# Attention's loop on Trainium2: a chunk's loads issued one a slot, those of an inverse one a step

## The chip, the cores and the metric

The kernel runs on one core of a Trainium2 chip. The metric is the device time of one execution in microseconds (us); the median of several executions is compared. A core has a matrix engine (TensorE, PE in the profile, with its weight loads as PEld), VectorE (DVE), ScalarE (ACT), GpSimd (POOL) and SyncE (SP), which here only issues DMAs. Each engine takes its instructions in the order of its own list and waits on semaphores for the others.

## The reference

Two layers, each an attention part and an MLP whose outputs are multiplied and added to the residual. The change lies in the first layer's attention, a gated delta rule over 1024 steps, for 2 sequences of 16 heads of 128:

```python
q, k, v = (silu(causal_dwconv(x @ W)) for each)      # k scaled by 128 ** -0.5
alpha, beta = sigmoid(x @ Wa + ba), sigmoid(x @ Wb + bb)
def step(S, inps):
    qt, kt, vt, at, bt = inps
    Sk  = einsum('bhvk,bhk->bhv', S, kt)
    err = Sk - vt
    S   = at[..., None, None] * S - bt[..., None, None] * (err[..., None] * kt[:, :, None, :])
    ot  = einsum('bhvk,bhk->bhv', S, qt)
    return (S, ot)
o = layernorm_over_128(o) * ln_w + ln_b
return (o * sigmoid(x @ Wg)) @ Wo
...
x = x + s * silu(ffn(xn))          # the first layer's end; a second layer follows
```

## The kernel before, in words

**Chunks.** The recurrence is done in 8 chunks of 128 steps. Four streams (two heads of two sequences, `NS`) form a head group `hg`, 8 of them; a unit is one head group and one chunk, 64 units in all, in an order that alternates two head groups. Within a chunk a unit lower triangular matrix has to be inverted. It is done by 32x32 diagonal blocks: `invert` loads those of all chunks of one head group into `ll` (four DMAs of 128 KB, in pieces of 32 numbers), sets `ml` to the identity (two POOL memsets), eliminates in 31 steps of two DVE instructions each (`tl`, then `ml`), copies the result back into `ll` in four ACT copies, and stores it with four DMAs. It is a generator: each `next` of it does one step.

**The loop.** After a front part (layernorm, the first MLP, the first three head groups' keys and decays, about 400 us) the loop `for u in range(len(units) + 1)` runs the units. `weave` cuts each unit into 10 slots (`LINKS`): a slot advances one of two chains (`across` of this unit or of the one before), runs what is due, and gives the wide projections (`made`, `ahead_k`) and the small products of `within` and `ahead_l` to the matrix engine up to a share of their summed cost. `later(n, *steps)` puts its steps off: the first by n slots, each following one by one slot more. Outside the loop it runs them at once.

**Order.** In the loop the instructions of PE, DVE, ACT and POOL are kept in the order in which the program writes them (`Ordered`). Those of `nc.sync`, all DMAs, are not: a scheduler places them into SP's list when the program is built, so that moving one in the source need not move it by as much in the list. SP's list is one list: a DMA whose semaphore has not come holds up all DMAs behind it, and each DMA also waits for the one eight places ahead of it to land.

**What a unit loads.** `within`, called for the next unit at the start of each, issues one DMA each for `kb` (keys), four for `ground` (the `G` blocks, the inverses, 40 KB each in pieces of 32 numbers), one for `eb` (decays) and one for `eg` (row decays, broadcast). `eg` and `kb` are read by POOL's products `kg` and `qg`, five slots later; `eb` by DVE's `kd` and `at`; `ground` by PE's products `zw` in the chain one unit later. The chain itself goes pks, `rt` (DVE), pr, `rr` (ACT), and then four times `zw` into `w` (ACT), with `rr` reduced by DVE in between; each `w` is turned into `wt` by four small DMAs (16 KB), the last by DVE copies. `pst` needs all of `wt`, and makes the next `state`.

**The inverse in the loop.** Every 8 units an inverse is started (u = 0, 8, 16, 24, 32, 40), and its steps are taken at fixed slots of 7 of the 8 units: four in the first unit (slots 0, 7, 8, 9), six in each other one (slots 0, 2, 4, 5, 7, 9), 40 in all:

```python
if u % 8 < 7:
    for k in (0, 2, 4, 5, 7, 9) if u % 8 else (0, 7, 8, 9):
        later(k + 1, lambda steps=steps: next(steps, None))
```

Before the change all four loads of `ll` and the memsets fall to the first step, two steps do nothing, and the elimination begins in the fourth.

Of the kernel before, what the change touches and what calls it, by code (L numbers as in the profile page):

```python
# [22 lines left out]
P = 128  # L23
# [7 lines left out]
NS = 4  # L31
# [25 lines left out]
def cols(ap, n):  # L57

    if len(ap.shape) == 2:
        ap = ap.unsqueeze(2)  # L60
    return ap.to_broadcast([ap.shape[0], ap.shape[1], n])
# [246 lines left out]
def first_layer(ctx, tc, a, cst, minus_half, keep, xnT, od, gd, pd, then):  # L308
# [29 lines left out]
    nc = tc.nc  # L338
# [223 lines left out]
    gr, egr = (dr.tile([NCOL, P], F32, name=n, bufs=1) for n in ("gr", "egr"))  # L562
# [10 lines left out]
    def rows(src, hg, c, dst):  # L573

        col = c * H * B + hg * NS
        nc.sync.dma_start(
            dst, src[col : col + NS, :].rearrange("s t -> (s t)").unsqueeze(0).to_broadcast([P, NS * P])
            .rearrange("p (s t) -> p s t", s=NS)
        )
# [6 lines left out]
    order = {"loop": False, "slot": 0}  # L586
# [6 lines left out]
    def later(n, *steps):  # L593


        for i, step in enumerate(steps):
            if order["loop"] and n + i:
                due.setdefault(order["slot"] + n + i, []).append(step)
            else:
                step()  # L600

    def mm(out, **kw):
        PE.matmul(out, **kw)

    def turn(out, src):
        PE.transpose(out, src, ident)
# [136 lines left out]
    def invert(hg, store):  # L743

        ll = pl.tile([P, 32, 32], F32, tag="ll", name=f"ll_{hg}")
        for bl in range(4):
            nc.sync.dma_start(
                ll[32 * bl : 32 * bl + 32],
                store["l"][:, :, :, SLOT[bl], :].rearrange("c s i t -> (c s) i t"),
            )  # L750
        m = pl.tile([P, 32, 32], F32, tag="ml", name=f"ml_{hg}")
        POOL.memset(m, 0.0)
        POOL.memset(m.rearrange("p i j -> p (i j)")[:, 0 : 32 * 32 : 33], 1.0)
        for _ in range(3):
            yield
        for i in range(31):
            shape = [P, 31 - i, i + 1]
            t = pl.tile([P, 256], F32, tag="tl", name=f"tl_{hg}_{i}", bufs=2)
            tv = t[:, : (31 - i) * (i + 1)].rearrange("p (t j) -> p t j", j=i + 1)
            DVE.tensor_tensor(  # L760
                tv,
                ll[:, i, i + 1 :].unsqueeze(2).to_broadcast(shape),
                m[:, i, : i + 1].unsqueeze(1).to_broadcast(shape),
                ALU.mult,
            )
            rest = m[:, i + 1 :, : i + 1]
            DVE.tensor_tensor(rest, rest, tv, ALU.subtract)
            yield

        for i in range(0, 32, 8):  # L770
            ACT.copy(ll[:, :, i : i + 8].rearrange("p j i -> p i j"), m[:, i : i + 8])
            yield
        for bl in range(4):
            nc.sync.dma_start(
                store["l"][:, :, :, SLOT[bl], :].rearrange("c s j i -> (c s) j i"),
                ll[32 * bl : 32 * bl + 32],
            )
        yield

    def within(hg, c, store):  # L780

        u = f"{hg}_{c}"
        half = slice((c % 2) * P, (c % 2 + 1) * P)
        q = windows[hg, c // 2]["q"][:, :, half]
        k = pools["b"].tile([P, NS, P], F32, tag="kb", name=f"kb_{u}")
        nc.sync.dma_start(k, store["k"][c // 2][:, :, half])
        G = pools["g"][:, units.index((hg, c)) % 3]
        for s in range(NS):
            r = slice(32 * s, 32 * s + 32)
            nc.sync.dma_start(G[r, :, r], store["l"][c, s])  # L790
        e = pools["b"].tile([P, NS, P], F32, tag="eb", name=f"eb_{u}", bufs=1)
        nc.sync.dma_start(e, store["e"][c])

        eg = pools["b"].tile([P, NS, P + 4], F32, tag="eg", name=f"eg_{u}", bufs=3)
        POOL.memset(eg[:, :, 0:1], 1.0)
        rows(egr, hg, c, eg[:, :, 1 : P + 1])
        kg = pools["b"].tile([P, NS, P], F32, tag="kg", name=f"kg_{u}")
        qg = pools["b"].tile([P, NS, P], F32, tag="qg", name=f"qg_{u}", bufs=3)
        later(
            5,  # L800
            lambda: POOL.tensor_tensor(kg, k, eg[:, :, 0:P], ALU.mult),
            lambda: POOL.tensor_tensor(qg, q, eg[:, :, 1 : P + 1], ALU.mult),
        )
        yield 0
        pk = pools["i"].tile([P, NS, P], F32, tag="pi", name=f"pk_{u}")
        for s in range(NS):
            turn(pk[:, s, :], k[:, s, :])

        kd = pools["b"].tile([P, NS, P], F32, tag="kd", name=f"kd_{u}", bufs=3)
        later(1, lambda: DVE.tensor_tensor(kd, pk, cols(e[:, :, P - 1 : P], P), ALU.mult))  # L810
        yield 4 * TURN

        pqk = pools["a"].tile([P, NS, P], F32, tag="pa", name=f"pqk_{u}")
        for s in range(NS):
            mm(pqk[:, s, :], lhsT=k[:, s, :], rhs=q[:, s, :], start=True, stop=True)
        at = pools["b"].tile([P, NS, P], F32, tag="at", name=f"at_{u}", bufs=3)
        later(1, lambda: DVE.tensor_tensor(at, pqk, e, ALU.mult))
        parts[hg, c] = eg, qg, kg, at, kd, G
        yield 4 * NARROW
# [156 lines left out]
    for hg in range(3):  # L976
        stores[hg] = new_store(hg)
        wk = load_weights(hg, ("wk",))
        steps = invert(hg - 1, stores[hg - 1]) if hg else iter(())
        for p in range(NP):  # L980
            for step in of_e:
                step()
            some(1)
            done(ahead_k(hg, p, wk["wk"], stores[hg]))
            loads, *of_e = ahead_e(hg, p, stores[hg])
            of_e = itertools.chain(*of_e)
            for step in loads:
                step()
            some(1)
            ell()  # L990
            for _ in zip(range(0 if hg and not p else 14), steps):
                pass
            ls.append((hg, p))
# [52 lines left out]
    with tc.issue_after(last["act"].ins):  # L1046
# [3 lines left out]
        done(made(0, 0, "v"))  # L1050
        done(made(1, 0, "q"))
        done(within(0, 0, stores[0]))
        halves = sorted(pd)

# [56 lines left out]
        for u in range(len(units) + 1):  # L1111
# [15 lines left out]
            if u % 8 == 0:  # L1127
                steps = invert(slot + 2, stores[slot + 2]) if slot + 2 < HG else none
                if slot + 3 < HG:
                    wk = load_weights(slot + 3, ("wk",))  # L1130
                    stores[slot + 3] = new_store(slot + 3)
# [12 lines left out]
            if u + 1 < len(units):  # L1144
                hg, c = units[u + 1]
                ready = within(hg, c, stores[hg])
                other(ready, 1)
# [4 lines left out]
            if turn4 in (0, 2) and ls:  # L1152
                hg, i_ = ls[turn4 // 2]
# [599 lines left out]
```

## Time and profile before

| what | value |
|---|---|
| median of 3 runs | 3177.61 us (3177.41 to 3177.93) |
| profiled execution | 3174.2 us, of which the span 3172.4 us |
| granted TensorE clock, mean | 0.999 |
| PE busy in the span | 3138.0 us |
| attention's loop in the trace | about 400 to 1825 us |
| DMAs of SP in the loop, per unit | 12 of `wt`, 4 of `ground`, one each of `kb`, `eb`, `eg` and others |

The span is the time from the first to the last instruction of the profiled execution. In the rows of the profile, nearly all lines are L132, the helper through which ordered instructions pass; so they are told apart by their tiles, written out<-in. PE's busy time is modelled at its end and says how long it was occupied, not how well; a wait is read from the idle time before an instruction and from what ended it.

### The profile page before, as it was taken

Reading aid. Unit: us, or ns where it says so; the run is one execution under the profiler, and the core shown is the slowest. Engines: PE = TensorE matmul, PEld = TensorE weight load, DVE = VectorE, ACT = ScalarE, POOL = GpSimd, SP = SyncE. Lnnn points to the kernel's source line nnn. Section 1 sums busy time; section 2 is a strip of 40 time slices with the busy share of each in tenths; the row PEclk is TensorE's granted clock in tenths of the full one; section 3 lists DMA queues with packets and bytes.
Section 4 is the critical chain, followed back from the end, with each engine's and each line's share of the span. In section 5 each row is a group of like instructions: output and inputs, shape, how many; then the busy total and the mean of one; then the engine's idle time right before and its main releaser. Section 6 shows DMA issues by size and latency. Waiting matters only on the chain.

```text
span 3172.4 us, 38119 instructions
## 1 busy us (share of the span) xinstructions
PE 3138.0 (99%) x12390; PEld 1941.4 (61%) x12390; DVE 2148.2 (68%) x4294; ACT 1251.4 (39%) x2269; POOL 833.4 (26%) x1210
## 2 busy tenths in 40 slices
PE   8999999999999999999999999999999999999998
PEld 7577756666666666666666644555555555555554
DVE  5557678786877868675545455677777666776677
ACT  3476555546555555534433311222222222322223
POOL 2000122222222222322222210333333333333322
PEclk9999999999999999999999999999999999999999
DMA  6244344444444543443334364100011001010014
GB/s 184 63 119 113 104 132 119 112 131 126 122 108 129 142 122 105 111 133 101 89 89 137 112 212 155 31 30 27 27 33 34 27 27 34 27 33 27 27 37 133
DMA packets 499751, 287.40 MB, mean 91 GB/s; under 512 B 207585, under 2 KB 440801, under 8 KB 499553
## 3 DMA queue, kind: packets, MB, share of 16 engines
q1 hardware_dynamic: 490688, 268.97, 30.0%
q0 software_dynamic: 6560, 11.80, 1.3%
q10 hardware_dynamic: 2304, 4.20, 0.4%
q8 instruction: 99, 1.62, 0.2%
q14 instruction: 100, 0.81, 0.1%
HBM read 183.90 MB, written 88.34 MB: 86 GB/s over the span
## 4 chain that ended last, share of the span: by engine, by line
PE 89%; DVE 5%; ACT 2%; issue 2%; DMA 1%; SPq 1%; POOL 0%; DVEq 0%; ACTq 0%; POOLq 0%
PE po L132 18%; PE pua L132 7%; PE pga L132 7%; PE pwk L132 6%; PE pgate L132 6%; PE pwv L132 5%; PE pwq L132 5%; PE jpo L211 4%; PE zw L132 4%; PE puc L132 3%; PE pgc L132 3%; PE pu L132 3%; PE pg L132 3%; PE pr L132 2%; PE pub L132 2%; PE pgb L132 2%
## 5 line engine op out<-in xcount | busy, mean ns | idle before, releaser
L132 DVE TENSOR_TENSOR acc<-acc,po 128x512 f32<-128x512 f32 x408 | 278.2, 682 | 208.3 <-PE po L132 207.6
L132 PEld LDWEIGHTS po<-w_d,i 128*128 128x128 f32 x1024 | 194.5, 190 | 142.6 <-issue 111.2
L132 PE MATMUL po<-w_d,i 128*128 128x256 f32 (+1 forms) x1024 | 275.4, 392 | 0.0
L132 PE MATMUL pgate<-xnT,wg 128*128 128x512 f32 x512 | 245.8, 593 | 0.2 <-ACT q L132 0.2
L132 PE MATMUL pwq<-xnT,wq 128*128 128x512 f32 x512 | 245.2, 594 | 0.0
L132 PE MATMUL pwv<-xnT,wv 128*128 128x512 f32 x512 | 243.0, 593 | 1.8 <-ACT gate L132 1.8
L132 PE MATMUL pua<-xq,w_u 128*128 128x512 f32 x512 | 240.6, 592 | 0.0
L132 PE MATMUL pga<-xq,w_g 128*128 128x512 f32 x512 | 240.6, 592 | 0.0
L132 PE MATMUL pwk<-xnT,wk 128*128 128x512 f32 x512 | 236.1, 593 | 1.7 <-ACT ka L132 1.7
L132 ACT COPY g<-pga 128x512 f32<-128x512 f32 x96 | 56.2, 585 | 445.8 <-PE pga L132 438.5
L132 DVE SCALAR_TENSOR_TENSOR v<-prewv,cw,v 128x512 f32<-128x512 f32 x192 | 166.3, 867 | 62.5 <-ACT v L132 53.1
L132 PEld LDWEIGHTS po<-w_d,s 128*128 128x128 f32 x720 | 136.8, 190 | 95.4 <-issue 76.8
L132 ACT COPY w<-zw 128x128 f32<-128x128 f32 x192 | 50.6, 264 | 356.7 <-PE zw L132 356.5
L132 DVE TENSOR_TENSOR rr<-rr,zw 128x128 f32<-128x128 f32 x192 | 54.8, 285 | 197.3 <-PE zw L132 193.3
L132 PE MATMUL po<-w_d,s 128*128 128x256 f32 x720 | 184.8, 379 | 0.0
L132 ACT ACT_TABLE_LOAD x133 | 170.6, 1283 | 17.8 <-PE pr L132 11.3
L132 POOL TENSOR_TENSOR rs<-rs,minus_half 128x4 f32<-128x4 f32 x64 | 64.5, 1007 | 427.0 <-DVE rs L132 409.2
L132 POOL TENSOR_TENSOR ot<-ot,gate 128x512 f32<-128x512 f32 x64 | 86.3, 1348 | 338.0 <-ACT ot L132 308.3
L132 DVE SCALAR_TENSOR_TENSOR ka<-prewk,cw,ka 128x512 f32<-128x512 f32 x192 | 149.6, 781 | 33.8 <-ACT ka L132 23.2
L132 PEld LDWEIGHTS zw<-rr,ground 128*128 128x128 f32 x512 | 96.5, 190 | 123.9 <-issue 102.4
L132 DVE SCALAR_TENSOR_TENSOR q<-prewq,cw,q 128x512 f32<-128x512 f32 x192 | 159.1, 829 | 15.7 <-POOL eg L132 7.3
L132 PEld LDWEIGHTS zw<-w,ground 128*128 128x128 f32 x768 | 110.9, 191 | 66.0 <-issue 55.4
(248 smaller groups left out, 6647.2 us busy)
## 6 DMA issues: line engine op xcount, KB each, us to landing
e<-gr SPq DMA_DIRECT2D x64, 256.0 KB, 3.9
de<-e SPq DMA_DIRECT2D x64, 256.0 KB, 2.9
dk<-ka SPq DMA_DIRECT2D x32, 512.0 KB, 2.8
kb<-dk SPq DMA_DIRECT2D x64, 256.0 KB, 3.4
eb<-de SPq DMA_DIRECT2D x64, 256.0 KB, 3.0
eg<-egr SPq DMA_DIRECT2D x64, 256.0 KB, 3.9
od<-ot SPq DMA_DIRECT2D x64, 256.0 KB, 2.1
wt<-w SPq DMA_DIRECT2D x768, 16.0 KB, 2.0
```

The costliest lines, as they stand in the source:

```text
L132: i = getattr(self.engine, name)(*args, **kw)
L211: matmul(po, lhsT=ot[:, h, :], rhs=self.wo[h], start=(h == h0), stop=(h == H - 1))
```

## The change

In `within`, `kb` stays where it was; the loads of `eg`, `eb` and the four of `ground` are put off to one a slot, in this order, from the next slot on. In `invert`, when it runs in the loop, each of the four loads of `ll` is a step of its own, and the empty steps go; the memsets fall to the step of the first elimination, the fifth, and everything after it comes one step later than before. Outside the loop nothing changes. In the diff no line of the output projection is touched.

```diff
@@ invert @@
                 ll[32 * bl : 32 * bl + 32],
                 store["l"][:, :, :, SLOT[bl], :].rearrange("c s i t -> (c s) i t"),
             )
+            if order["loop"]:
+                yield
         m = pl.tile([P, 32, 32], F32, tag="ml", name=f"ml_{hg}")
         POOL.memset(m, 0.0)
         POOL.memset(m.rearrange("p i j -> p (i j)")[:, 0 : 32 * 32 : 33], 1.0)
-        for _ in range(3):
+        for _ in range(0 if order["loop"] else 3):
             yield
@@ within @@
-        for s in range(NS):
+        e = pools["b"].tile([P, NS, P], F32, tag="eb", name=f"eb_{u}", bufs=1)
+
+        eg = pools["b"].tile([P, NS, P + 4], F32, tag="eg", name=f"eg_{u}", bufs=3)
+        POOL.memset(eg[:, :, 0:1], 1.0)
+
+        def block(s):
             r = slice(32 * s, 32 * s + 32)
             nc.sync.dma_start(G[r, :, r], store["l"][c, s])
-        e = pools["b"].tile([P, NS, P], F32, tag="eb", name=f"eb_{u}", bufs=1)
-        nc.sync.dma_start(e, store["e"][c])
-
-        eg = pools["b"].tile([P, NS, P + 4], F32, tag="eg", name=f"eg_{u}", bufs=3)
-        POOL.memset(eg[:, :, 0:1], 1.0)
-        rows(egr, hg, c, eg[:, :, 1 : P + 1])
+
+        later(
+            1,
+            lambda: rows(egr, hg, c, eg[:, :, 1 : P + 1]),
+            lambda: nc.sync.dma_start(e, store["e"][c]),
+            *(functools.partial(block, s) for s in range(NS)),
+        )
```

## The prediction

> **What bounds the kernel now.** I read the page first, then the window sums, then PE's waits, then the order of time around the longest of them.
>
> The page says that the matrix engine is never free: PE is busy 99% of the span, and 89% of the chain that ended last is PE's.
>
> ```profile
> PE 3138.0 (99%) x12390; PEld 1941.4 (61%) x12390; DVE 2148.2 (68%) x4294; ACT 1251.4 (39%) x2269; POOL 833.4 (26%) x1210
> PE 89%; DVE 5%; ACT 2%; issue 2%; DMA 1%; SPq 1%; POOL 0%; DVEq 0%; ACTq 0%; POOLq 0%
> ```
>
> The window sums give the loop (400 to 1825 us) by itself; the columns are busy us of PE, PEld, DVE, ACT, POOL.
>
> ```profile
> 400.00:1825.00 1425.00, 1411.22 (x6766) 909.58 (x6765) 986.77 (x2429) 698.47 (x1423) 385.34 (x664) 1.00 0.43 117
> ```
>
> So PE was idle 1425.0 - 1411.2 = 13.8 us there. Busy PE can hide a wait, so I also took the distance from each matmul's start to the next, less the median of its shape (429 ns for 128x512, 111 ns for 128x128): 27.6 us in excess over the loop, of which 17 us lie in places of over 0.15 us. That is a ceiling: a change that leaves PE's list alone cannot win more than 27 us (0.9%). And it does leave it alone: with buffer numbers left out, the built program has the same list on PE. PE's waits in the loop say what little is to be had:
>
> ```profile
> PE pst L132 <- DMA wt<-w: 3.5, 1, 3.5
> PE pst L132 <- DVE wt L132: 2.9, 3, 1.7
> PE pwv L132 <- ACT gate L132: 1.8, 3, 0.6
> PE zw L132 <- ACT w L132: 1.7, 4, 1.1
> PE zw L132 <- DVE rr L132: 1.0, 3, 0.5
> ```
>
> One of them is a DMA's. It is at u = 40, where an inverse starts and the unit is short because no keys are prepared any more. SP's and PE's timelines there (start, duration, what):
>
> ```profile
> 1315.84 1.84 SPq L735 DMA_DIRECT2D dl<-lt  x4
> 1318.30 2.71 SPq L747 DMA_DIRECT2D ll<-dl  x4
> 1321.06 2.97 SPq L790 DMA_DIRECT2D ground<-dl  x4
> 1324.12 0.55 SPq L792 DMA_DIRECT2D eb<-de  x1
> 1324.72 0.43 SPq L576 DMA_DIRECT2D eg<-egr  x1
> 1325.25 4.97 SPq L868 DMA_DIRECT2D wt<-w  x8
> ...
> 1328.87 1.13 PE L132 MATMUL pst<-wt,kd 128*128 128x128 f32 x8 [3.52 <-DMA wt<-w]
> ```
>
> ACT's `w` for the first of these `wt` was ready at 1317.4, but its DMAs stood behind fourteen others until 1325.25: PE stood from 1325.4 to 1328.9. At the starts of u = 8 to 32 the same queue forms, but PE has more other work and waits for no DMA.
>
> **The change part by part.** Each DMA costs SP about 0.6 us of issue, wherever it stands; none is added or taken away. In the built program's order SP has 2122 DMAs as before.
>
> *SP's order at an inverse's start.* At u = 40 it becomes: four `dl`, one `ll`, `kb`, `eg`, `eb`, four `wt`, three `ground`, four `wt`, `ll`, `ground`, two `ll`. From the row above: first `ll` issued by 1318.9, then three DMAs, so `wt` from about 1320.7 to 1323.1, landing (2.0 us median) by 1325.1, when PE wants it at 1325.6. The wait for the DMA goes. What is late next is `wt`'s last quarter, which DVE copies: in the trace these copies end at 1326.3, behind two taps that wait for ACT until 1323.45. `pst` would start at 1326.3 and not 1328.87: 2.6 us. But `eg` lands at about 1324 and not 1328.6, and so POOL's `kg` starts then, beside the second of those taps.
>
> *A rule that speaks against the change.* DVE at the place of PE's longest wait for DVE (`wt`, 1.84 us at 1236.5), with POOL beside it:
>
> ```profile
> 1233.52 0.37 DVE L132 TENSOR_TENSOR ml<-ml,tl 128x207 f32<-128x207 f32 x1
> 1235.56 2.86 DVE L132 SCALAR_TENSOR_TENSOR v<-prewv,cw,v 128x512 f32<-128x512 f32 x2 [1.67 <-ACT v L132]
> 1238.45 1.25 DVE L132 COPY wt<-zw 32x128 f32<-32x128 f32 x4
> ...
> 1235.08 1.29 POOL L132 TENSOR_TENSOR kg<-kb,eg 128x512 f32<-128x512 f32 x1
> 1236.32 1.55 POOL L132 TENSOR_TENSOR qg<-q,eg 128x512 f32<-128x512 f32 x1
> ```
>
> Two taps take 2.86 us, where two take 1.54 with POOL free (1323.45). Of the loop's 504 taps the 401 with no large POOL product beside them take 0.76 us at most; the 103 with one have a median of 1.17. [...] I take 0.6 (half a pair's loss, since the tap may have begun first): 2.0 us is left.
>
> *The loads of a unit elsewhere.* `eg` comes earlier in SP's list in 28 units, by up to 10 places, because it no longer stands behind `ground`; `ground` comes later for 101 of its 256 DMAs, by up to 20; `kb` later in 15 units, by up to 6; `wt` earlier for 188 of 768. Set at the times of their new places, `ground` still lands 8.7 us or more ahead of the first `zw` that reads it, `eb` 4.9 ahead of `kd`, `kb` 3.5 ahead of its reader. So these cost nothing; the cover is that slack, and without it PE's `zw` would wait by what is missing. POOL's waits show what the earlier `eg` is worth on POOL:
>
> ```profile
> POOL kg L132 <- DMA eg<-egr: 24.2, 10, 6.8
> ```
>
> Yet nobody waits for `kg`: PE's list of waits has none. Worth 0, except by the collisions, which move in ten units and can fall well or badly.
>
> *The inverse.* Its first elimination comes one step later and its loads three steps later. Two DVE instructions (0.39 us at 612.0) leave the place ahead of `rr`; PE waited there for `rr` at 794.1 (0.70 us) and 435.5 (0.23): -0.4 and -0.2. They go to behind `at`, ahead of `rt` at u = 8, 24, 40; ahead of them other DVE work is shorter by as much, so `rt` is not later by them. But the fourth `ll` now lands shortly before. At u = 8 and 24 it is issued at 611.2 and 972.1 at the latest (the `wt` before it at its old time, then five DMAs), and lands 3.9 us after its issue began: 615.1 and 976.0, with `at` over at 615.9 and 976.7. No wait. At u = 40: `wt` until 1327.5, then four DMAs, issued from 1329.5, landed by 1333.4 to 1334; there `at` is over, with the 2.0 us gained, at about 1334. A wait of 0 to 1.8 us, and `rt` with PE's `pr` right behind: I take +0.3. [...] At u = 16 and 32 the fourth load may be some tenths late, but no `rt` follows there.
>
> The two memsets (1.17 us of POOL) move 15 places, behind a copy that ends at 611.5 at u = 8, so they are over by 612.7, ahead of 615.9: 0. Without that gap of 3 us DVE, with `rt` behind, would wait for POOL. ACT's four copies at an inverse's end (0.65 us each) come one step later, and the four stores up to 5 places later; PE has no wait of over 0.15 us in those units, and the stores are read over a unit later: 0, with ±0.6 for each of six if an ACT copy hits a `w`.
>
> **Sum.** -2.0 (u = 40) - 0.6 (`rr`) + 0.3 (`ll`) = -2.3 us. The profiled execution is 3174.2 us (span 3172.4 and 1.8 around it) and would become 3171.9. The median is 3177.6, 3.4 above it; the same step gives 3175.3.
>
> **The rivals.** About 0.2% (6.4 us) is what a measurement of this kernel can tell from no change, so the forecast is "within".
>
> *More is won (faster).* If `wt` early and POOL free early ease the DVE waits also, most of the 17 us in single places is open: u = 40 with its whole 3.7, the 1.8 at 1236, 0.9 at 1409, 0.7 at 1751 and the start's 1.0 make 8.1: 3169.5. For it: `kg` waited for a DMA ten times, and `wt` moves forward. Against: the waits for ACT (`gate`, `w`) repeat at fixed places that SP does not touch, and at 1236 SP's order is unchanged.
>
> *Collisions (slower).* `kg` and `qg`, started earlier in units where `eg` was late, fall on taps ahead of `wt` copies, as at 1236. Price: 1.8 us each by that row. It decides from five such units on (5 x 1.8 - 2.3 = +6.9 us); with all ten it is +16: 3193. With six, 3186. Against: DVE is idle 438 of 1425 us in the loop, and only taps in front of a PE wait count.
>
> *It does nothing.* SP's scheduler had already pulled the old loads apart in most units; then only u = 40 changes, and if the taps collide there, the result is 3177.6.
>
> **How the numbers follow.** The likeliest case with the third rival, 0.60: 3171.5 to 3183. More is won by over 6.4 us, 0.17. Collisions, or an ACT or `ll` wait I have undersized, by over 6.4 us, 0.23. The range for 8 in 10 is 3168 to 3186: it takes in part of both outer cases.
>
> **What would show it.** Right: no PE wait for `wt`'s DMA near 1325, `pst` there at about 1327, `kg<-eg` waits well below 24 us, PE's idle time in the loop near 12 us. Wrong: a DVE wait for `ll` at the first `tl` of u = 8 or 24, new PE waits for `wt` copies or `rr` with a tap of over 1 us ahead of them, or PE waiting for `ground`.

## The result, and the profile after

| | before | after |
|---|---|---|
| median, runs of the first comparison (20 each) | 3177.47 us (3173.73 to 3180.52) | 3171.31 us (3169.64 to 3173.70) |
| ratio | | 0.9985 [0.9979, 0.9990] |
| profiled execution | 3174.2 us (span 3172.4) | 3172.0 us (span 3170.2) |
| all runs with a granted clock on record | 3176.12 (n = 110, standard deviation 1.95) | 3171.36 (n = 31, 1.20) |

The 110 are without before's 20 of the first comparison, whose clock is not on record; with them its median is 3176.17. So the change makes the kernel faster by 6.2 us in the first comparison and by 4.8 us over all runs (interval 4.0 to 5.5). The forecast was 3175.3 us, 2.3 us below before. The first thing to see is that the two profiled executions differ by 2.2 us only, nearly the forecast. The one of before, at 3174.2, is a short one: of 130 executions of that kernel 17 are shorter. The question was therefore twofold: are the steps of the sum where they were said to be, and where do the other 2.5 to 4 us come from, which this pair of profiles doesn't show?

On the page of after PE's busy time is 3136.5 us, 1.5 less, and its share stays 99%.

The window sums of after give the loop: PE idle 1425.0 - 1412.8 = 12.2 us, where 12 had been forecast.

```profile
400.00:1825.00 1425.00, 1412.79 (x6774) 911.60 (x6773) 992.52 (x2439) 698.14 (x1423) 383.58 (x666) 1.00 0.43 118
```

PE's waits in the loop of after (what waits, for what: us in total, times, longest). The wait for the DMA of `wt`, 3.5 us, is gone. DVE's copies have one wait more (4.7 in 4, it was 2.9 in 3), and `w` has 3.5 us in 7, where it had 1.7 in 4.

```profile
PE pst L132 <- DVE wt L132: 4.7, 4, 1.7
PE zw L132 <- ACT w L132: 3.5, 7, 1.1
```

**u = 40.** The timeline of after there (start, duration). SP's order is the one forecast. `wt` is issued from 1320.26, and `pst` starts at 1326.86, where it had waited until 1328.87. But `eg` lands at about 1323, so `kg` and `qg` now run beside the two taps (a tap is a DVE instruction that adds one step of the causal convolution), which take 3.20 us and not 1.54. What PE waits for, 1.74 us, is the `wt` copies behind these taps.

```profile
1320.26 2.44 SPq L876 DMA_DIRECT2D wt<-w  x4
...
1323.29 3.20 DVE L132 SCALAR_TENSOR_TENSOR v<-prewv,cw,v 128x512 f32<-128x512 f32 x2 [3.02 <-ACT v L132]
...
1323.16 1.28 POOL L132 TENSOR_TENSOR kg<-kb,eg 128x512 f32<-128x512 f32 x1 [0.33 <-DMA eg<-egr]
1324.40 1.54 POOL L132 TENSOR_TENSOR qg<-q,eg 128x512 f32<-128x512 f32 x1
...
1326.86 1.46 PE L132 MATMUL pst<-wt,kd 128*128 128x128 f32 x8 [1.74 <-DVE wt L132]
```

**u = 32.** Here the change made a wait that was not there. The timeline of after: `kg` starts 5.6 us earlier than in before (1148.33 there, after a wait of 3.96 us for `eg`) and meets a pair of taps, which take 2.81 us instead of 1.54. `w` then comes late, and PE's `zw` waits for it.

```profile
1142.78 1.30 POOL L132 TENSOR_TENSOR kg<-kb,eg 128x512 f32<-128x512 f32 x1
...
1143.32 2.81 DVE L132 SCALAR_TENSOR_TENSOR v<-prewv,cw,v 128x512 f32<-128x512 f32 x2 [2.36 <-ACT v L132]
...
1151.27 0.71 PE L132 MATMUL zw<-w,ground 128*128 128x128 f32 x4 [1.10 <-ACT w L132]
```

**The drift.** PE's list is the same in both kernels, so each product of one can be set against the same product of the other. The difference of their start times, after less before, is the drift; where it steps, time was won or lost. The table has the steps of three profiled executions of the changed kernel's lists against the one of before; the third has two waits filled, as told below. Negative is faster.

| stretch of the loop (us) | what | after | after again | after filled |
|---|---|---|---|---|
| 419 to 425 | `pr`, first unit | -0.24 | -0.98 | -1.06 |
| 425 to 440 | `rr` at 436 | -0.33 | -0.33 | -0.33 |
| 440 to 690 | `rr` at 442, `pr` at 687 | -0.75 | -0.73 | -0.75 |
| 790 to 800 | `rr` at 795 | -0.80 | -0.81 | -0.81 |
| 800 to 850 | sundry | -0.63 | -0.62 | -0.62 |
| 1140 to 1155 | `zw` for `w`, u = 32 | +1.27 | +1.26 | +1.26 |
| 1239 to 1245 | behind the wait of u = 36 | 0.00 | +1.33 | +0.01 |
| 1245 to 1326 | ending in `pst`, u = 40 | -1.71 | -2.37 | -2.07 |
| stretches not listed, in sum | | +0.21 | +0.40 | +0.42 |
| whole loop (395 to 1830) | | -2.98 | -2.85 | -3.95 |

Most steps repeat to 0.02 us from one execution to the next. Three do not: the first unit's, u = 40's, and one of 1.33 us at 1240, behind a wait that both kernels have. The experiments are about these. Executions differ ahead of the loop too, in kernels with and without the change: by -1.0 to +1.0 us at 395 against the first one of before. After had +0.5 there and +0.3 behind the loop, which is why the two profiles differ by 2.2 us and their loops by 3.0.

### The profile page after: what moved, and what is told of

Same layout as the page of the kernel before. It is cut to its first block, busy times and chain, and to the rows that moved or that the text cites. A ratio compares the mean times of both kernels' runs of the same rounds, so it can differ in the third digit from the quotient of the medians.

```text
span 3170.2 us, 38109 instructions
## 1 busy us (share of the span) xinstructions
PE 3136.5 (99%) x12390; PEld 1941.8 (61%) x12390; DVE 2151.2 (68%) x4294; ACT 1251.1 (39%) x2269; POOL 830.9 (26%) x1210
## 4 chain that ended last, share of the span: by engine, by line
PE 88%; DVE 5%; issue 2%; ACT 2%; DMA 2%; SPq 1%; POOL 0%; DVEq 0%; ACTq 0%; POOLq 0%
PE po L132 17%; PE pua L132 7%; PE pga L132 7%; PE pgate L132 6%; PE pwk L132 6%; PE pwq L132 5%; PE pwv L132 5%; PE jpo L211 4%; PE zw L132 4%; PE puc L132 3%; PE pgc L132 3%; PE pu L132 3%; PE pg L132 3%; PE pr L132 2%; PE pub L132 2%
```

## The experiments

The kernels ran in three groups of four, each on a chip of its own and with its own runs of before: medians 3176.05, 3176.13 and 3175.79 us (33 runs each).

### The two kernels again

> The kernel before, unchanged, for its profile. Its first profiled execution took 3174.2 us, 3.3 below its median of 3177.5, and stood only 2.2 us of span above the one of the changed kernel, while the medians are 6.2 apart. If the missing 4 us are waits that the kernel before has in most executions and missed in that one, a profiled execution near 3177.5 shows them as steps of PE's drift against the changed kernel, most likely at the starts of an inverse (u = 8 to 40), where SP's queue is longest. If they lie outside the loop (front, second layer), the steps stand before 400 or behind 1825 us, and the change has nothing to do with them. Time: ratio 1.000 to the kernel before.

> The changed kernel, unchanged, on the same chip as the others: 0.9985 of the kernel before, and a profile with pst at u = 40 waiting for DVE's wt (about 1.9 us) and not for a DMA, and the wait for w at u = 32 (1.26 us) again, since both come from the order of kg and the taps and not from chance.

Measured: before 3176.45 us, ratio to its neighbours 1.0001 [0.9992, 1.0010]; after 3171.42, 0.9986 [0.9978, 0.9995]. The difference is there again, 4.6 to 5 us, and the profile of before was 3176.9 this time, 2.7 us above the first. This second profile shows where an ordinary execution of before is longer. The window sums of before over the stretch behind the wait of u = 40, and then of before again over those behind u = 36 and u = 40; the third column from the right is PE's granted clock, which the first profile of before has at 1.00 behind u = 36 too.

```profile
1328.00:1336.00 8.00, 7.13 (x55) 6.39 (x56) 5.87 (x13) 1.32 (x2) 4.37 (x6) 1.00 0.25 75
```

```profile
1236.00:1243.00 7.00, 5.32 (x17) 3.07 (x17) 6.38 (x16) 2.88 (x4) 2.18 (x5) 0.76 0.43 103
1328.00:1336.00 8.00, 6.82 (x35) 6.85 (x36) 4.66 (x12) 0.97 (x2) 3.91 (x6) 0.57 0.30 86
```

The clock's records in that trace say the same: half of full speed for 3.4 us from 1239.7 and for 6.8 us from 1328.4. In the timeline of before again `pst` takes 2.05 us behind the wait, where the row shown of before has 1.13, though nothing in the lists has changed:

```profile
1329.18 2.05 PE L132 MATMUL pst<-wt,kd 128*128 128x128 f32 x8 [3.48 <-DMA wt<-w]
```

The drift of this execution against the first one of before grows by 1.34 us at 1240 and by 2.25 us between 1326 and 1340. The first profile of before had the same two waits (1.68 and 3.52 us) and no half clock behind either: whether a wait draws one differs from one execution to the next, and no run here shows what decides it. Of the 11 profiles of this study in which the wait at u = 36 is as it was (1.67 to 1.73 us), four have half clock for 3.4 us behind it. Over the loop, the first profile of before was the lucky one.

### One part of the change alone

Only what `within` does; in `invert` the old order stands:

```diff
-            if order["loop"]:
-                yield
...
-        for _ in range(0 if order["loop"] else 3):
+        for _ in range(3):
```

> Only the loads of a chunk are put off; the inverse's four loads stay in one step. At u = 40 wt stands behind four dl, four ll, kb, eg and eb and is issued from about 1322.9 on, landed by 1327.2; eg lands near 1326, behind the two taps, so kg does not meet them: pst at about 1327.2 (1328.87 before, 1326.86 with the whole change in the trace's own times). The new wait of 1.26 us at u = 32 (kg beside the taps) stays if eg lands before 1145 there. Theory of the queue: 2 to 4 us of the 6 us. Rival, that the loads of ll are what counts: nothing.

Measured: 3172.22 us, ratio 0.9989 [0.9980, 0.9998], 3.9 us below all runs of before (interval 2.0 to 5.3). `pst` at u = 40 starts at 1325.49, after a wait of 1.83 us, and `kg`, at 1324.50, comes behind the pair of taps, as expected. The profile names DVE's `wt` as what ended the wait, but those copies were over at 1324.57. The first of the `wt` DMAs, issued at 1321.07, landed at 1325.41: what is left is still a wait for a DMA. The step at 1151 is there (+1.13), and the `rr` step at 795 is smaller (-0.4 over 790 to 800).

Only what `invert` does; in `within` the old order stands:

```diff
-        later(
-            1,
-            lambda: rows(egr, hg, c, eg[:, :, 1 : P + 1]),
-            lambda: nc.sync.dma_start(e, store["e"][c]),
-            *(functools.partial(block, s) for s in range(NS)),
-        )
+        for s in range(NS):
+            r = slice(32 * s, 32 * s + 32)
+            nc.sync.dma_start(G[r, :, r], store["l"][c, s])
+        nc.sync.dma_start(e, store["e"][c])
+        rows(egr, hg, c, eg[:, :, 1 : P + 1])
```

> Only the inverse's loads are spread and its steps moved. At u = 40 ground still stands ahead of wt and waits for PE until 1321.9, then eb and eg: wt from about 1325, as before, pst at about 1328.9. No collision at u = 32. The wait for rr at 794 (0.70 us) goes, since tl and ml left its place. Theory of the queue: 0.5 to 1.5 us gained. Rival, that the loads of ll count: 4 to 6 us.

Measured: 3175.08 us, ratio 0.9997 [0.9988, 1.0006], 1.0 us below all runs of before (interval 0.0 to 2.0). There are two misses. The first is at u = 40. The put-off `ll` alone brings `wt` forward enough, `pst` at u = 40 starts 1.9 us earlier, although this execution reached the place 1.4 us later, and the wait for the DMA that is left is 0.5 us. The timeline of this kernel there shows why it needs no more: `eg` stays behind `ground`, so `kg` starts after the taps, which take 1.54 us.

```profile
1324.61 1.54 DVE L132 SCALAR_TENSOR_TENSOR v<-prewv,cw,v 128x512 f32<-128x512 f32 x2 [3.02 <-ACT v L132]
...
1326.85 1.30 POOL L132 TENSOR_TENSOR kg<-kb,eg 128x512 f32<-128x512 f32 x1 [2.71 <-DMA eg<-egr]
...
1327.01 1.13 PE L132 MATMUL pst<-wt,kd 128*128 128x128 f32 x8 [0.50 <-DMA wt<-w]
```

Its drift then comes back to zero. The second miss is at u = 32, where no collision was expected: `kg` meets the pair of taps here too (2.45 us), and `zw` waits 0.74 us for `w` (+0.9). PE also waits for ACT's `v` at 849.6 and 1211.5 (0.60 and 0.54 us), which it does neither in before nor in after; why was not followed up. The execution had the half clock at 1240 (+1.33), and lost 0.5 us by 1340 and 1.3 more by 1412. Each part alone shortens the long wait, to 1.83 and 0.50 us; that the one is worth 3.9 us and the other 1.0 lies elsewhere.

### Is it the clock? Waits filled with work

If the half clock behind a wait is the missing time, then a kernel that waits as long, but keeps PE busy meanwhile, must win it. In before, products are put ahead of `pst` at u = 40 that are overwritten by it:

```diff
+            if order["loop"] and (order["slot"] - 1) // LINKS == 40:
+                for s in list(range(NS)) * 3:
+                    mm(pst[:, s, :], lhsT=kd[:, s, :], rhs=kd[:, s, :], start=True, stop=True)
             for s in range(NS):
                 mm(pst[:, s, :], lhsT=kd[:, s, :], rhs=wt[:, s, :], start=True, stop=True)
```

> Kernel before, with one addition: ahead of pst at u = 40, where PE waits 3.5 us for wt's DMAs, twelve more products of kd by kd (128x128, about 0.22 us each, 2.7 us together) are written into pst and then overwritten by it. They lengthen nothing: they lie inside the wait. Theory A (the granted clock: a wait of 3.5 us draws a stretch at half clock of up to 6.8 us right behind it, in most executions, and that is the part of the gain that the profiled spans don't show): PE stays busy, the wait left over is 0.8 us, the profile shows no half clock near 1328, and the median is 2 to 3.4 us below before, though pst starts when it did. Theory B (the time is only that of the waits): pst starts when it did, and the median is that of before, within 0.7 us.

Measured: 3175.87 us, ratio 0.9996 [0.9987, 1.0005]. The filling lies where it should, as PE's timeline of this kernel shows; PE's idle time is gone but for 0.25 us, and `pst` starts when it did but for half a microsecond:

```profile
1325.26 2.84 PE L132 MATMUL pst<-kd 128*128 128x128 f32 x24
1328.35 1.13 PE L132 MATMUL pst<-wt,kd 128*128 128x128 f32 x8 [0.25 <-DMA wt<-w]
```

The mean granted clock of an execution tells more than the median. Of the 11 executions one was at 0.998 and none below; of the 110 of before 34 were at 0.998 and 21 at 0.997. But the median came down by 0.25 us only (interval 1.7 less to 0.4 more), the mean by 0.8. So the median is where Theory B has it. Theory A was right on what draws the half clock and expected too much of it. A possible reason is seen in the profile of before again: u = 36 draws one too. So both waits were filled, in both kernels:

```diff
+            if order["loop"]:
+                for i in range({36: 6, 40: 12}.get((order["slot"] - 1) // LINKS, 0)):
+                    mm(pst[:, i % NS, :], lhsT=kd[:, i % NS, :], rhs=kd[:, i % NS, :], start=True, stop=True)
```

In before these are six products at u = 36 and twelve at u = 40; in after, six at each.

> Kernel before with both of PE's longest waits filled: ahead of pst at u = 36 six, and at u = 40 twelve more products of kd by kd, about 0.22 us each, written into pst and then overwritten by it. All lie inside the waits (1.7 and 3.5 us). Theory A (clock and waits share the difference): no half clock at 1239 or 1329, every execution at a mean granted clock of 0.999, the median 0.8 to 1.5 us below before, the spread between executions narrower. Theory B (the clock costs nothing that counts): the median of before, the same spread.

> Kernel after with the same two waits filled (six products of kd by kd each, 1.3 us of 1.7). With no half clock left in either kernel, this and before with its waits filled differ by the waits alone. Theory A: 0 to 0.5 us below after, 3 to 3.7 us below the filled before, which is what the drift of the two kernels' products in the loop shows (2.9). Theory B: the whole 4.8 us stays between the filled kernels.

| | granted clock 0.997 | 0.998 | 0.999 or more | median (us) | standard deviation |
|---|---|---|---|---|---|
| before, all runs | 21 (mean 3178.8) | 34 (3177.0) | 55 (3175.0) | 3176.12 | 1.95 |
| before, both filled | 0 | 0 | 11 | 3174.69 | 1.14 |
| after, all runs | 0 | 5 (3171.8) | 26 (3171.4) | 3171.36 | 1.20 |
| after, both filled | 0 | 0 | 11 | 3171.15 | 0.73 |

With the waits filled no execution of either kernel stands below 0.999, and the spread is smaller in both. The mean is a coarse measure: two profiles of this study (the inverse's part alone, and the first kernel of the last section) stand at 0.999 with one stretch of 3.4 us in them. For before the columns are clear all the same: 55 of 110 executions below 0.999, 1 of 11 with the wait of u = 40 filled, none of 11 with both. For after, 5 of 31 against none of 11 can be chance. The long wait is not the whole of it either: with `within`'s part alone, 5 of 11 executions stand at 0.998.

Filled before lies 1.4 us below before (0.2 above to 2.2 below), filled after 0.2 below after (0.5 above to 1.2 below). Between the filled kernels 3.5 us are left (interval 2.9 to 5.1), against 4.8 between the unfilled. The means of the last clock column say much the same: 3175.0 - 3171.4 = 3.6 us. So my estimate is that about 1.2 of the 4.8 us is clock, and about 3.5 is waits. It is not more than an estimate: the intervals leave room for a share of the clock from nothing to 2 us, Theory B's 4.8 lies inside the interval of the 3.5, and the profiles of the two filled kernels, without half clock in the loop, are 4.6 us apart there. What the columns do show is that in before executions with a lower clock are longer, and that filling the waits takes the lower clock away.

The stretches of half clock in these profiles last 3.4 or 6.8 us and come in some executions and not in others. One of them came behind a wait of 1.68 us (the one that ends at 1238 in before again), so by the rows a forecast would have to count this wait as well as the one of 3.5 us.

### The change at u = 40 alone, and everywhere else

```diff
+        put_off = order["loop"] and (order["slot"] - 1) // LINKS == 40
...
-            if order["loop"]:
+            if put_off:
                 yield
...
+        if order["loop"] and (order["slot"] - 1) // LINKS == 40:
+            later(1, *loads)
+        else:
+            for load in (*loads[2:], loads[1], loads[0]):
+                load()
```

The second kernel has `!= 40` in both places. `loads` are those of `eg`, `eb` and `ground`, in that order.

> The change made only in what is put off at u = 40 (the loads of the unit prepared there and of the inverse started there); everywhere else the loads stand as before. Theory A (waits and clock): the wait for wt's DMA falls to about 1.7 us of DVE's copies, pst starts about 1.8 us earlier, no half clock follows near 1328, and the median is 4 to 5 us below before, nearly all of the whole change. Theory B (only waits count): 1.8 us below. Theory C (the gain is spread over many units): under 1 us.

> The change made everywhere but at u = 40. PE's wait for wt's DMA near 1328 stays at 3 to 3.5 us. Theory A (waits and clock at u = 40 carry it): 0 to 1 us below before (rr at 794 with 0.7, some tenths at 421 and 436, less 1.3 at u = 32). Theory C (the gain is spread over many units): 3 to 5 us below.

> The change made only at u = 40, a second time, since the gains of it (1.7 us) and of the change everywhere but there (0.4) had not added up to that of the whole change (4.6 to 6.2). If that was chance: 2.5 to 3.5 us below before now, with pst at u = 40 earlier by about 1.8 us. If the parts help each other: 1.2 to 2 us below again, and the profile shows the gain at u = 40 given back within the next five units.

Measured: only u = 40 3174.40 us, and 3174.31 the second time, together 1.7 us below before (0.9 to 2.5); everywhere else 3175.75, 0.4 below (3.0 below to 1.5 above), with the long wait at u = 40 still there and, in its profile, half clock for 3.4 us from 1330.0. The expectation of 4 to 5 us from u = 40 was wrong; that of the second run, 1.2 to 2 us with the gain given back behind, came true. The two kernels' gains don't add up to 4.8, though the interval of the 0.4 is over 4 us wide. The traces account for two pieces of the gap.

First, the gain at u = 40 is partly given back, in both profiles of the kernel that has only it: 1.1 us by 1412. PE waits 0.27 us for `rt` at 1397 and 0.85 for `rr` at 1405. The timeline of the second shows the latter, and a collision of DVE's `tl` with POOL's `ot` ahead of both: `tl` takes 1.50 us, where in after it takes 0.41. In after, `ot` starts 2.5 us earlier and meets taps that have more room; there the second wait is 0.32 us and the first is not there. That the collision makes these waits is read from the order in time, not tested.

```profile
1404.66 0.49 PE L132 MATMUL zw<-rr,ground 128*128 128x128 f32 x2 [0.85 <-DVE rr L132]
...
1390.22 1.50 DVE L132 TENSOR_TENSOR tl<-ll,ml 128x252 f32<-128x252 f32 x1
...
1389.66 1.78 POOL L132 TENSOR_TENSOR ot<-ot,gate 128x512 f32<-128x512 f32 x1 [9.40 <-ACT ot L132]
```

Second, both kernels leave out something that I had not seen as part of the change. The section on the change above says that nothing changes outside the loop. That is not so: the first unit's `within` runs before the loop, where `later` issues at once, and so in the new order, with `eg` first; these two kernels have the old order there. `kg` also stands three instructions earlier in POOL's list. SP, POOL, DVE and PE of before around the loop's start:

```profile
406.93 0.43 SPq L576 DMA_DIRECT2D eg<-egr  x1
...
411.38 1.28 POOL L132 TENSOR_TENSOR kg<-kb,eg 128x512 f32<-128x512 f32 x1 [6.80 <-DMA eg<-egr]
...
409.17 2.33 DVE L132 SCALAR_TENSOR_TENSOR v<-prewv,cw,v 128x512 f32<-128x512 f32 x3 [1.37 <-ACT v L132]
412.74 3.27 DVE L132 SCALAR_TENSOR_TENSOR q<-prewq,cw,q 128x512 f32<-128x512 f32 x3 [1.24 <-POOL prewq L132]
...
420.97 0.66 PE L132 MATMUL pr<-cst,rt 128*128 128x128 f32 x4 [0.85 <-ACT rt L132]
```

`kg` waits for `eg`, and behind it in POOL's list stands the memset of `prewq`, for which DVE's taps of `q` wait 1.24 us; `qg` falls on these taps, which take 3.27 us (2.32 in after again, where it doesn't), ACT's `q` and `rt` follow, and PE's `pr` waits 0.85 us. The same in after again: `eg` is issued three microseconds earlier, `kg` starts 3.6 earlier, and `pr` starts at 419.92 without a wait.

```profile
403.92 0.61 SPq L576 DMA_DIRECT2D eg<-egr  x1
...
407.81 1.29 POOL L132 TENSOR_TENSOR kg<-kb,eg 128x512 f32<-128x512 f32 x1 [7.59 <-DMA eg<-egr]
...
409.43 3.30 DVE L132 SCALAR_TENSOR_TENSOR v<-prewv,cw,v 128x512 f32<-128x512 f32 x3 [1.90 <-POOL prewq L132]
412.64 2.32 DVE L132 SCALAR_TENSOR_TENSOR q<-prewq,cw,q 128x512 f32<-128x512 f32 x3
```

The collision is not gone: `qg` now meets the taps of `v`, which take 3.30 us and not 2.33, and those of `q` are free. Both groups together take as long as before (5.62 and 5.60 us). What is won, about 1 us, is waiting: DVE stood 1.37 us for ACT and 1.24 for POOL ahead of them, and stands 1.90 us now; and the taps ahead of both had ended 0.3 us earlier.

Over 419 to 425 the drift steps by -0.24 to -1.07 us in the six profiles of kernels with the new order at the first unit (the median is -1.0), and by -0.03 to +0.61 in those with the old order but one: with the inverse's part alone it is -0.66, and why was not followed up. No kernel changed this order alone, so the amount is read from traces and not tested by itself. With it, 1.7 + 0.4 + 1.0 + 1.1 makes 4.2 of the 4.8 us; what is left is well within what these medians can tell.

### The collisions, taken away

In after, `kg` and `qg` are put off further where they had met the taps; first in every eighth unit, then at u = 32, 36 and 40 alone:

```diff
         later(
-            5,
+            8 if order["slot"] % (8 * LINKS) < LINKS and order["loop"] else 5,
             lambda: POOL.tensor_tensor(kg, k, eg[:, :, 0:P], ALU.mult),
```

> Kernel after, with POOL's kg and qg put off by eight slots and not five in the units prepared at u = 8, 16, 24, 32 and 40. Theory: the pair of taps at u = 32 (2.81 us) and at u = 40 (3.20 us) lost 1.3 and 1.6 us to kg and qg; with these later they take about 1.54 each, the wait of zw at 1151 (1.1 us) goes, pst at u = 40 starts 1.3 to 1.6 us earlier: 2 to 3 us below after. Rival: the taps or the copies then meet the products elsewhere, or the next unit's pks waits for kg: no gain, or some us lost.

```diff
-            5,
+            8 if order["loop"] and (order["slot"] - 1) // LINKS in (32, 36, 40) else 5,
```

> Kernel after, with POOL's kg and qg put off by eight slots and not five in the units prepared at u = 32, 36 and 40 alone. Theory: the taps ahead of the copies of wt at u = 36 take 1.54 us and not 2.86, pst there starts 1.3 us earlier and draws no half clock; with u = 32 and 40 as in the kernel that did it at every eighth unit (-0.9 us in the median) the median is 1.5 to 2.5 us below after. Rival: the products then fall on the taps behind (rr, state), and as much is given back as at u = 40 (1.1 us): -0.5 to -1.

Measured: 3170.50 and 3170.44 us, together 0.9 us below after (interval 0.3 to 1.5). The second has a ratio to before of 0.9980 [0.9972, 0.9989], the lowest median of the study, and a standard deviation of 0.50 us; all executions of both stand at a clock of 0.999. The collisions are what they had been taken for: the step of +1.26 us at 1151 is gone, and the timeline of the first of these kernels has the taps at u = 40 at 1.54 us again and `pst` at 1323.96, without a wait. But the next product behind it now waits for `rr`, because `kg` runs beside the tap ahead of `rr`, which takes 1.85 us, where a single tap takes 0.75 with no POOL product beside it:

```profile
1322.05 1.54 DVE L132 SCALAR_TENSOR_TENSOR v<-prewv,cw,v 128x512 f32<-128x512 f32 x2 [3.02 <-ACT v L132]
...
1324.91 1.85 DVE L132 SCALAR_TENSOR_TENSOR v<-prewv,cw,v 128x512 f32<-128x512 f32 x1
...
1324.91 1.29 POOL L132 TENSOR_TENSOR kg<-kb,eg 128x512 f32<-128x512 f32 x1
...
1327.13 0.49 PE L132 MATMUL zw<-rr,ground 128*128 128x128 f32 x2 [1.27 <-DVE rr L132]
```

So of the 3 us that the two places have in the trace about a third is kept. The expectations of 2 to 3 and of 1.5 to 2.5 us were too high; the second one's rival, that as much is given back behind, was right. The second kernel's `pst` at u = 36 waits 0.40 us and not 1.7, and no half clock follows in its profile; but 13 us later `pr` waits 1.06 us for `rt`, which it does not in after. In the profile of the first kernel, which leaves the wait of u = 36 as it was, half clock does follow, at 1237.

## Why the prediction was right, and where its sum was off

The forecast, no change that can be told (-2.3 us, within 6.4), holds, if narrowly: it was -4.8 over all runs and -6.2 in the first comparison, and 3171.3 us lies inside the range of 3168 to 3186, though just below the 3171.5 with which the likeliest case began. The sign and the main place are as argued. That the sum comes near the loop's -3.0 is in part luck: 1.4 us in steps that it did not have (440 to 690 and 800 to 850) and 0.5 more at `rr` stand against 1.3 lost at u = 32, a collision that it had left at 0. Step by step:

- *u = 40, forecast -2.0.* Right in mechanism: -1.7, -2.4 and -2.1. The size came out by two errors that cancel. The DMA wait went, and the next to be late was `wt`'s last quarter behind two taps. The half pair of collision (0.6) was the author's estimate, for a tap that has begun ahead of `kg`; in after `kg` starts first (1323.16, the taps at 1323.29). It was too little: the taps lost 3.20 - 1.54 = 1.66 us, a full pair and more, above the row's 1.3; at u = 32 it was 2.81 - 1.54 = 1.27, as the row has it. Against that, the sum let `pst` start when all four copies of `wt` are over (1326.3), a gain of 2.6 us. It starts behind the first of them (copies from 1326.52, `pst` at 1326.86), and without the collision the whole wait of 3.5 us goes, as the kernels with `kg` put off show (a step of -3.52 in both).
- *`rr`, forecast -0.6.* 0.3 at 436 and 0.8 at 795: -1.1, nearly twice as much. Steps of a few tenths at 442, 687 and 828 (-0.7 over 440 to 690, -0.6 over 800 to 850) were not in the sum at all; what makes each of them was not followed up.
- *Fourth `ll`, forecast +0.3.* No wait at u = 40: its issue ended at 1329.94 and the first `tl`, at 1333.46, follows `at` at once. (The 3.9 us to landing that the prediction took are the median of `ll` in before's list of DMAs; after's has 4.1.) The one wait of DVE for it is at u = 16 (1.6 us, at 794.8), where the prediction had "some tenths", and it cost PE nothing: no `rt` follows there.
- *`kg`'s wait for `eg`, forecast "well below 24 us" and worth 0.* This is the step that failed. The waits fell to 18.9 us only (POOL's waits of after):

```profile
POOL kg L132 <- DMA eg<-egr: 18.9, 9, 7.0
```

  And the sentence "nobody waits for `kg`" looked at readers of `kg` alone. At the first unit the memset of `prewq` stands behind `kg` in POOL's list, and DVE's taps wait for that. Its gain of up to 1 us at the loop's start is the largest gain in one place that the sum lacked. The prediction named "the start's 1.0" only under the rival *More is won*.
- *Collisions.* The rival's price of 1.8 us a unit was 1.26 at u = 32; it was to decide from five such units on (5 x 1.8 - 2.3 is 6.7, not the 6.9 written there), and besides u = 40 there was one new one that reached PE.
- *The clock.* The sum had no term for it. The prediction put the median at the profiled execution's change (-2.3) on the assumption that the 3.4 us between that execution and the median would stay. They didn't: part of it was half clock, much of it behind the very wait that the change removes, and went with the wait; about 1.2 us by the estimate above.
- *It does nothing* is ruled out by the ratio's interval; *More is won*, with its 8.1 us, overshot, though it came closer to the first comparison than the forecast did.

## What to carry to other kernels

When a wait of PE is removed, count its own length, and look in a second execution of the same kernel at what the clock does behind it: here, in some executions and not in others, waits of 1.7 and 3.5 us cost 1.3 and 2.2 us more in the products that followed. When an engine's instruction gets its data earlier, ask not only who reads its result but what stands behind it in that engine's list, and which instruction of another engine it will now run beside. And a profile is one execution: where its time lies at the edge of the runs' range, the difference of two profiles is not the difference of the medians.

## What the runs showed of the hardware

- The granted clock fell to half behind waits of PE of 1.7 us at u = 36 (in 4 of 11 profiles) and of 3.5 to 3.9 us at u = 40 (in 2 of 3), in stretches of 3.4 or 6.8 us; the waits of 1.3 to 1.8 us that other kernels have at u = 40 drew none in five profiles. The half clock comes in some executions and not in others of the same kernel (half of before's 110 have a mean clock of 0.998 or 0.997). Filling the waits with products that nobody reads took the lower clock of before away (none of 11), and made neither kernel slower: the medians came down by 1.4 and 0.2 us, both with intervals that take in zero.
- A `scalar_tensor_tensor` tap on DVE beside a POOL product of 128x512: a pair of taps took 2.81, 2.86 and 3.20 us, where it takes 1.54 alone; a single one 1.85, where it takes 0.75.
